# Adding the residual by TensorE and moving the softplus by one unit in a four-layer selective-scan kernel

## The chip, the cores and the metric

The kernel runs on one core of a Trainium2 chip as one program. The metric is the device time of that program in microseconds, the median of several executions. Besides the times there is one execution taken with the hardware profiler, and every duration below is of that one.

## The reference, cut to what matters

The input is a batch of 8 images with 192 channels and 56 x 56 points. Four layers follow each other, each `x = x + layer(group_norm(x))`. Layer 0 is an involution, layer 1 three narrow selective scans per image, and layers 2 and 3, which the change touches, one wide selective scan each:

```
xz = in_proj(group_norm(x));  x_in, z = split(xz)          # 384 channels each
xc = silu(conv4(x_in) + conv_b)                            # causal, along the points
dt, B, C = split(x_proj(xc));  dt = softplus(dt_proj(dt) + b)
h[d,n,t] = exp(dt[d,t]*A[d,n]) * h[d,n,t-1] + dt[d,t]*xc[d,t]*B[n,t]     # n < 16
y[d,t]   = sum_n C[n,t]*h[d,n,t] + D[d]*xc[d,t]
x = x + out_proj(y * silu(z))
```

## The kernel before, in words

**Jobs and units.** An image is cut into 7 chunks of 448 points. In layers 2 and 3 one chunk is one *job*, so there are 56 jobs in each. A job has 3 groups of 128 channels (j), and a group has 4 *units* (q), so 12 units, numbered 0 to 11 here (m in the code). A unit works on a tile `uhg` of 128 partitions x 4 x 449 numbers and takes these steps, each on its own engine:

- `decays` (L764): ScalarE writes exp(dt*A) into PSUM, in two halves of 2 activations. Each half has one buffer, so the decays of unit k+1 wait for the scan of the same half of unit k.
- the *product* dt*xc*B: by VectorE (`inputs_by_vector`, L792), which reads B from a PSUM tile that TensorE spreads (`spread_b`, L752), or by GpSimd (`inputs_by_pool`, L785), which reads B from a tile `rows` that a DMA brings (`row_in`, L649). `pool_units` says which units GpSimd has; in layers 2 and 3 these are 1, 3, 7, 9 and 11, and VectorE has the other seven.
- two *scans* (L796), one per half, on VectorE.
- the *readout* (L805): GpSimd multiplies the states by C. `keep` (L800) and `inputs_begin` (L772) carry the last state over on ScalarE.
- `reduce` (L814): TensorE adds up over n; at the first unit of a group also L811 (D*xc). After a group VectorE multiplies by the gate (`gated`, L830).

**The order.** Nothing is scheduled by a tool: the loop over units in `ssm_layer` writes each engine's order by hand. In iteration k VectorE does scan (k, 0), the product of k+1, scan (k, 1); GpSimd is given the product of k+2 and then the readout of k-2; TensorE is given the reduction of k-3 first. So the engines work on different units at the same time, each strictly in its own order. In unit 4 VectorE also does the product of unit 6 (`switches`).

**The background work.** What the next job needs is laid into 24 *places* of the running job, two for each unit: place 2m runs ahead of scan (m, 0) and place 2m+1 ahead of scan (m, 1). `places` spreads each list of steps evenly over a stretch of places by their costs; `bounds` gives the stretches. The input and convolution matmuls (L1136, L1168) stand in places 0 to 7; the block that swaps ScalarE's function table, does the two silus and swaps back (L616, L597, L589) in place 8; then the output projection of the job before (`after`, L1188) with the residual add on VectorE (L1194), and the projection to dt, B and C (L621, evicted by L625 and L626); the deltas (L655, L660) and the split of B into bf16 parts (L632, L633, L637) in places 10 to 13; in place 14 the softplus block, again between two table loads (L663, L589). The matmuls L667 bring xc into PSUM, VectorE makes dt*xc with them (`dtx`, L670), and `store` (L674) sends both to DRAM. From place 18 on come the write of the finished chunk, the normalization of the next and the gate matmuls. A *step* has matmuls and a rest; the rest waits in a list until a later step flushes it. Where a unit has little of this, TensorE is given matmuls of zeros (`nothing`, L820).

**The DMA queue.** All DMAs of these layers are issued by SyncE, in one order. A group's operands are fetched back from DRAM with each row repeated four times, by four DMAs (`load_ops`, tile `rep`, L742). They wait for the store of that group to land (`ops`, L674). The three `rows` of the next job that GpSimd's products need (`row_in(0, 1..3)`) are issued in units 9, 10 and 11, at the start of the iteration:

```
row_in(0, m - (per_job - NQ))      # before: rows 1, 2, 3 in units 9, 10, 11
```

In layers 2 and 3 that places the first of them on SyncE's queue behind the store of group 0 of the next job, its four `rep` loads and the stores of groups 1 and 2. The tiles `rows` and `rep` have 4 and 2 buffers.

**PSUM.** The general matmul tiles (`mm_tile`) have two buffers; B, y and each half of the decays have their own.

Of the kernel before, what the change touches and what calls it, by code (L numbers as in the profile page):

```python
# [18 lines left out]
CP = 96  # L19
NCT = 2  # L20
RC = 8
T = RC * WW
# [17 lines left out]
class Step:  # L40


    def __init__(self, matmuls, rest, left, cost=None, block=False):
        self.matmuls, self.rest, self.left, self.block = matmuls, rest, left, block
        self.cost = cost if cost is not None else 1.0 if matmuls else 0.3
        self.closes = block
        self.settles = False


def pause(cost=1.0):  # L50
# [36 lines left out]
def conv_mamba_stack(ctx: ExitStack, tc: tile.TileContext, a, out):  # L87
    nc = tc.nc
# [15 lines left out]
    def mm_tile():  # L104
        return banks.mm.tile([128, 512], F32, tag="mm", name="mm")
# [16 lines left out]
    ident = const([128, 128], a["ident"])  # L122
# [589 lines left out]
    def ssm_layer(pool, w, jobs, n_slots):  # L712


        nd = w.nd
        units = [(i, j, q) for i in range(len(jobs)) for j in range(nd) for q in range(NQ)]
        groups = [(i, j) for i in range(len(jobs)) for j in range(nd)]
        per_job = nd * NQ

        def pool_units(i):  # L720

            if nd == 4:
                last = i + 1 == len(jobs)
                if jobs[i][0] == 0:
                    return {1, 3, 5, 7, 9, 11, 13, 15} if last else {1, 3, 6, 7, 10, 11, 13, 15}
                return {1, 3, 7, 9, 11, 13, 15} | ({5} if last else set())
            return {1, 3, 7, 9, 11} | ({6} if i + 1 == len(jobs) else set())

        pool_rows = (1, 2, 3)
        us = [Layer() for _ in jobs]  # L730
# [102 lines left out]
        def bounds(job):  # L833

            silu = 8 if nd == 3 else 6
            softplus = silu + (6 if nd == 3 else 8 if job[0] == 1 else 12)
            copies = silu + (4 if nd == 4 else 2)
            return (0, silu), (silu, silu + 2), (silu + 2, copies), (copies, softplus), (softplus, softplus + 1), (softplus + 2, softplus + 4), (softplus + 4, n_places)

# [46 lines left out]
        for k, (i, j, q) in enumerate(units):  # L886
            m = k % per_job
            if m == 0:

                fetch, outs, rest = tail  # L890
                if i + 1 < len(jobs):
                    u = us[i + 1]
                    at = bounds(jobs[i + 1])
                    stretches = *jobs[i + 1][2](u, us[i], outs), rest + jobs[i + 1][3](u)
                    plan = places(*((steps, *p) for steps, p in zip(stretches, at)))
                else:
                    gates = Step(None, lambda: with_gates(lambda: None, us[i]), 0, 0.3, block=True)
                    plan = places(([gates], 4, 6), (outs + rest, 8, n_places))
                plan[3][:0] = [Step(None, fetch, 2, 0.0)]

            if i + 1 < len(jobs) and m - (per_job - NQ) in pool_rows:
                us[i + 1].row_in(0, m - (per_job - NQ))
            if i and m < NQ:
                us[i].row_in(1, m)
            if k >= NQ + 3 and q == 3:
                gated(k // NQ - 1)
            switches = i + 1 < len(jobs) and m == at[1][0] // 2
            melts = nd == 4 and i + 1 < len(jobs) and jobs[i][0] == 0 and m == at[4][0] // 2
            opens = nd == 4 and k >= 3 and units[k - 3][2] == 0
            more = 3 - math.ceil(load_of(plan[2 * m] + plan[2 * m + 1]))  # L910
            if opens:
                bg.run(plan[2 * m])
            if k >= 3 and not melts:
                reduce(k - 3)
                nothing(k - 3, more > 2)
            if not opens:
                bg.run(plan[2 * m])
            if not melts:
                nothing(k - 3, more > 0)
            load_when_free(k)  # L920
            scan(k, 0)
            if k + 1 < n_units:
                decays(k + 1, 0)
            if k + 3 < n_units:
                inputs_begin(k + 3)
            if k + 2 < n_units:
                inputs_by_pool(k + 2)
            if k >= 2:
                readout(k - 2)
            if k + 1 < n_units:  # L930
                inputs_by_vector(k + 1)
            if nd == 3 and k + 2 < n_units:
                spread_b(k + 2)
            if nd == 4 and (switches or melts):
                spread_next_b(k + 1)
            if melts:
                reduce(k - 3)
                nothing(k - 3, (more > 2) + (more > 0))
            bg.run(plan[2 * m + 1])
            if nd == 4:  # L940
                spread_next_b(k + 1)
            nothing(k - 3, more > 1)
            load_when_free(k)
            scan(k, 1)
            if (switches or melts) and k + 2 not in by_pool:
                inputs_by_vector(k + 2)
            keep(k)
            if k + 1 < n_units:
                decays(k + 1, 1)
            if m == per_job - 1:  # L950
                tail = jobs[i][4](us[i])
# [174 lines left out]
    def dense_jobs(pool, w, layer):  # L1126
        jobs = []
        chunks = Chunks(pool, layer)
        cks = chunks.all
        for ck in cks:  # L1130
            c = ck.c

            def in_mm(m, ck=ck):
                pm = mm_tile()
                for k in range(NCT):
                    nc.tensor.matmul(  # L1136
                        pm[:, :T], lhsT=w.inw[:, k, m * 128 : (m + 1) * 128], rhs=ck.v[:, k, :],
                        start=(k == 0), stop=(k == NCT - 1),
                    )
                return pm  # L1140

            def norm(ck=ck):
                def gnorm():
                    ck.v = chunks.normalized(ck, "v", 2)

                return [Step(None, gnorm, 2), Step(None, lambda: chunks.fetch_next(ck), 2)]

            ck.norm = norm

            def prepare(u, *beside, c=c, ck=ck, in_mm=in_mm):  # L1150
                xps = {}

                def xin(j):
                    xps[j] = in_mm(j)

                def xin_out(j):
                    if j == 0:
                        ck.xin = pool.tile([128, w.nd, T + 3], F32, tag="xin", name="xin", bufs=2)
                        if c == 0:
                            nc.gpsimd.memset(ck.xin[:, :, 0:3], 0.0)  # L1160
                        else:
                            nc.scalar.copy(ck.xin[:, :, 0:3], cks[ck.place - 1].xin[:, :, T : T + 3])
                    evict(w, ck.xin[:, j, 3:], xps[j][:, :T], j)

                def conv_mm(j):
                    pm = mm_tile()
                    for k in range(4):
                        nc.tensor.matmul(pm[:, :T], lhsT=w.convd[:, j, k, :], rhs=ck.xin[:, j, k : k + T], start=(k == 0), stop=(k == 3))  # L1168
                    return pm

                convs, *others = project_steps(pool, w, u, conv_mm, 4, *beside)
                return (
                    (ck.norm() + [pause()] if ck.place == 0 else [])
                    + [Step(lambda j=j: xin(j), lambda j=j: xin_out(j), 1 if j else 0, 2) for j in range(w.nd)]
                    + convs, *others,
                )

            def gates(u, ck=ck, in_mm=in_mm):
                normed = cks[ck.place + 1].norm() if ck.place + 1 < len(cks) else []
                return normed + gate_steps(pool, w, u, lambda j: in_mm(w.nd + j), 2)  # L1180

            def after(u, ck=ck):
                ops = {}

                def out_proj(t):
                    ops[t] = mm_tile()
                    for j in range(3):
                        nc.tensor.matmul(  # L1188
                            ops[t][:CP, :T], lhsT=w.outw[:, j, t * CP : (t + 1) * CP], rhs=u.zs[:, j, :],
                            start=(j == 0), stop=(j == 2),  # L1190
                        )

                def add(t):
                    nc.vector.tensor_add(ck.x[:, t, :], ck.x[:, t, :], ops[t][:CP, :T])  # L1194

                return (
                    lambda: chunks.fetch_again(ck), [Step(lambda t=t: out_proj(t), lambda t=t: add(t), 1, 3) for t in range(NCT)],
                    [pause()] + chunks.leave_steps(ck),
                )

            jobs.append((0, c == 0, prepare, gates, after))
        return jobs

# [86 lines left out]
```

## Time and profile before

| what | us |
|---|---|
| median of 3 runs | 24391.19 |
| lowest, highest | 24375.81, 24401.58 |
| the profiled execution, its time | 24428.22 |
| its span (first to last instruction) | 24426.4 |
| VectorE busy | 23026.9 (94%) |
| GpSimd busy | 22738.4 (93%) |
| TensorE busy | 20547.5 (84%) |
| ScalarE busy | 17006.8 (70%) |
| layer 2, from 16705 to 20627 | 3922, of which VectorE 3674.7, GpSimd 3555.5, TensorE 3285.8, ScalarE 2892.3 busy |
| layer 3, from 20627 to 24407 | 3780, of which VectorE 3594.9, GpSimd 3545.4, TensorE 3243.2, ScalarE 2839.3 busy |

The profile gives busy time per engine, the costliest groups of instructions with what ended the idle time before them, the chain of work that ended last, and the DMA queues. The trace behind it can be asked for a timeline of one engine, for groups of instructions in a stretch of time, and for who waited for whom. An f32 matmul stands in it as two records. In the names, `uhg<-rep,rows` means that the instruction writes uhg and reads rep and rows; DVE is VectorE, ACT ScalarE, POOL GpSimd, PE TensorE, SPq SyncE's queue.

### The profile page before, as it was taken

Reading aid. Unit: us, or ns where it says so; the run is one execution under the profiler, and the core shown is the slowest. Engines: PE = TensorE matmul, PEld = TensorE weight load, DVE = VectorE, ACT = ScalarE, POOL = GpSimd, SP = SyncE. Lnnn points to the kernel's source line nnn. Section 1 sums busy time; section 2 is a strip of 40 time slices with the busy share of each in tenths; the row PEclk is TensorE's granted clock in tenths of the full one; section 3 lists DMA queues with packets and bytes.
Section 4 is the critical chain, followed back from the end, with each engine's and each line's share of the span. In section 5 each row is a group of like instructions: output and inputs, shape, how many; then the busy total and the mean of one; then the engine's idle time right before and its main releaser. Section 6 shows DMA issues by size and latency. Waiting matters only on the chain.

```text
span 24426.4 us, 238439 instructions
## 1 busy us (share of the span) xinstructions
PE 20547.5 (84%) x74445; PEld 6487.3 (27%) x74445; DVE 23026.9 (94%) x15882; ACT 17006.8 (70%) x32578; POOL 22738.4 (93%) x6775
## 2 busy tenths in 40 slices
PE   8988888888888888888888888888888887888888
PEld 2222222222222222222222222222333332333332
DVE  8989999999999999999999999997999998999999
ACT  2137777777777777777777777776777776777777
POOL 5669999999999999999999999997999998999999
PEclk9987888878887887887887887878989898999998
DMA  4433333333333333333333333333444443444443
GB/s 111 109 106 131 128 126 133 127 127 130 132 128 126 131 128 125 132 130 125 130 128 126 130 130 128 128 129 111 140 141 142 141 139 123 142 144 144 142 143 129
DMA packets 1209092, 3171.55 MB, mean 130 GB/s; under 512 B 166444, under 2 KB 470596, under 8 KB 1207688
## 3 DMA queue, kind: packets, MB, share of 16 engines
q1 hardware_dynamic: 1205016, 3155.25, 39.4%
q8 instruction: 584, 9.57, 0.2%
q14 instruction: 692, 5.67, 0.1%
q10 hardware_dynamic: 2800, 1.06, 0.0%
HBM read 2438.45 MB, written 555.55 MB: 123 GB/s over the span
## 4 chain that ended last, share of the span: by engine, by line
DVE 35%; PE 29%; ACT 14%; issue 11%; POOL 6%; DMA 5%; SPq 1%; DVEq 0%; POOLq 0%; ACTq 0%
DVE uhg L796 22%; DVE uhg L792 8%; ACT da L764 6%; PE y L814 4%; POOL uhg L805 4%; DMA rows<-bc 3%; PE mm L1110 3%; PE mm L1168 3%; PE mm L655 2%; PE mm L1080 2%; PE mm L621 2%; POOL uhg L785 2%; PE mm L429 2%; ACT dt L663 1%; PE y L820 1%
## 5 line engine op out<-in xcount | busy, mean ns | idle before, releaser
L796 DVE TENSOR_TENSOR_SCAN uhg<-da,uhg 128x898 f32<-128x898 f32 x8064 | 15913.4, 2011 | 606.9 <-ACT da L764 586.1
L805 POOL TENSOR_TENSOR uhg<-uhg,rows 128x1792 f32<-128x1792 f32 x4032 | 14730.5, 3674 | 283.6 <-ACT carry L800 267.4
L764 ACT ACTIVATE da<-rep,k 128x448 f32<-128x448 f32 x16128 | 10262.3, 636 | 1436.8 <-DVE uhg L796 1064.1
L785 POOL TENSOR_TENSOR uhg<-rep,rows 128x1792 f32<-128x1792 f32 x1795 | 7160.6, 3989 | 784.6 <-DMA rows<-bc 435.6
L814 PE MATMUL y<-uhg,k 128*32 128x448 f32 x32256 | 4516.4, 634 | 343.1 <-POOL uhg L805 341.4
L792 DVE TENSOR_TENSOR uhg<-rep,b 128x1792 f32<-128x1792 f32 x2237 | 4469.6, 1998 | 180.2 <-PE b L752 132.4
L800 ACT COPY carry<-uhg 128x4 f32<-128x4 f32 x4032 | 784.5, 195 | 3506.5 <-DVE uhg L796 3427.8
L820 PE MATMUL y<-w_d,k 128*128 128x448 f32 (+1 forms) x5280 | 2490.5, 575 | 0.0
L811 PE MATMUL y<-xc,w_d 128*128 128x448 f32 x2016 | 1533.4, 856 | 1091.2 <-DVE zs L830 1091.1
L1098 PE MATMUL mm<-xs,k 64*128 64x448 f32 x1344 | 875.4, 755 | 773.5 <-ACT zs L694 587.5
L655 PE MATMUL mm<-dbl,w_dt 36*128 36x448 f32 (+1 forms) x2016 | 1319.6, 753 | 222.4 <-ACT k L637 222.4
L814 PEld LDWEIGHTS y<-uhg,k 128*32 128x32 f32 x32256 | 679.9, 114 | 3093.6 <-issue 1935.2
L820 PEld LDWEIGHTS y<-w_d,k 128*128 128x128 f32 x5280 | 1023.1, 210 | 1645.0 <-issue 1618.3
L1136 PE MATMUL mm<-v,w_in 96*128 96x448 f32 x2688 | 1284.0, 612 | 80.3 <-ACT zs L696 36.8
L752 PE MATMUL b<-k,k 96*128 96x448 bf16 x2237 | 852.2, 381 | 446.5 <-DVE uhg L792 446.3
L1080 PE MATMUL mm<-xs,k 128*128 128x448 f32 x2688 | 1155.1, 571 | 26.3 <-ACT zs L694 11.3
L667 PE MATMUL mm<-xc,k 128*128 128x448 f32 x2016 | 1033.1, 630 | 84.4 <-DVE dt L670 84.4
L1168 PE MATMUL mm<-xin,w_conv 128*128 128x448 f32 x2688 | 1088.6, 547 | 1.4 <-ACT xin L696 0.8
L441 DVE TENSOR_TENSOR prod<-mm,shifted 128x448 f32<-128x448 f32 x1680 | 930.0, 613 | 152.5 <-PE mm L429 77.0
L811 PEld LDWEIGHTS y<-xc,w_d 128*128 128x128 f32 x2016 | 470.7, 270 | 1941.0 <-DVE zs L830 1375.2
L449 POOL TENSOR_TENSOR x<-x,one 96x448 f32<-96x448 f32 x560 | 630.7, 1134 | 265.3 <-DVE one L441 247.8
L621 PE MATMUL mm<-xc,w_x 128*36 128x448 f32 (+1 forms) x2016 | 816.4, 546 | 10.5 <-ACT xc L616 10.5
(138 smaller groups left out, 19388.1 us busy)
## 6 DMA issues: line engine op xcount, KB each, us to landing
rep<-ops SPq DMA_DIRECT2D x4032, 448.0 KB, 5.8
ops<-dt SPq DMA_DIRECT2D x1008, 448.0 KB, 3.2
rows<-bc SPq DMA_DIRECT2D x1960, 224.0 KB, 6.3
shifted<-xpad SPq DMA_DIRECT2D x672, 179.0 KB, 4.5
xg<-stream SPq DMA_DIRECT2D x168, 336.0 KB, 7.7
xr<-stream SPq DMA_DIRECT2D x168, 336.0 KB, 7.0
stream<-xr SPq DMA_DIRECT2D x112, 336.0 KB, 7.5
xs<-xg SPq DMA_DIRECT2D x224, 112.0 KB, 2.3
```

The lines of the kernel that those rows point to most:

```text
L621: nc.tensor.matmul(u.ps[:nk, :T], lhsT=w.xproj[:, j, :], rhs=u.xc[:, j, :], start=(j == 0), stop=(j == nd - 1))
L655: nc.tensor.matmul(u.dps[j][:, :T], lhsT=w.dtw[:, j * 128 : (j + 1) * 128], rhs=u.dbl[:nk, :], start=True, stop=True)
L764: nc.scalar.activation(t[:, 64 + 449 * r : 512 + 449 * r], reps[k // NQ][:, 2 * h + r, 0, :], AF.Exp, scale=w.neg_a[:, j * NR + 2 * h + r, ...
L785: nc.gpsimd.tensor_mul(uhg[k][:, :, 1:], reps[k // NQ][:, :, 1, :], b)
L792: nc.vector.tensor_mul(uhg[k][:, :, 1:], reps[k // NQ][:, :, 1, :], b)
L796: nc.vector.tensor_tensor_scan(v, banks.da[h][:, 63:961], v, 0.0, ALU.mult, ALU.add)
L805: nc.gpsimd.tensor_mul(v, v, us[i].rows[1, q].unsqueeze(1).to_broadcast([128, NR, T]))
L811: nc.tensor.matmul(ys[k // NQ][:, :T], lhsT=w.dd[:, j, :], rhs=us[i].xc[:, j, :], start=True, stop=False)
L814: nc.tensor.matmul(y[32 * r : 32 * r + 32, :T], lhsT=fold, rhs=uhg[k][:, r, 1:], start=False, stop=(q == NQ - 1))
L820: nc.tensor.matmul(ys[k // NQ][:, : nd * 112], lhsT=zeros, rhs=w.dd.rearrange("p j e -> p (j e)")[:, : nd * 112], start=False, stop=False,)
L1080: nc.tensor.matmul(pm[:, :T], lhsT=w.inconv[:, k, j * 128 : (j + 1) * 128], rhs=ck.xs[:, i, 2 - 2 * k : 2 - 2 * k + T], start=(k == 0), st ...
L1168: nc.tensor.matmul(pm[:, :T], lhsT=w.convd[:, j, k, :], rhs=ck.xin[:, j, k : k + T], start=(k == 0), stop=(k == 3))
```

## The change

In layers 2 and 3 alone:

- The residual is added by TensorE: two matmuls of `ident` with the chunk (f32, 96 x 96 x 448) open the two PSUM tiles of the output projection, at the start of place 8 (`ahead`), and ScalarE copies the finished tiles out (`leave`) where VectorE added before. For the last job, which nothing follows, they stand in `out_proj`.
- The softplus block goes from place 14 to place 16, that is from unit 7 to unit 8. The deltas and the split of B now have places 10 to 15. The products with xc and the stores follow in places 18 and 19 (before 16 and 17), and the last stretch begins with place 20.
- GpSimd has the product of unit 10 and VectorE that of unit 9 (before the other way round).
- `row_in` of the next job is called one unit earlier, in units 8, 9 and 10. By that the first two rows stand on SyncE's queue ahead of the store of group 0 and the `rep` loads, and the third behind the stores.

What follows from the planner: 209 more matmuls of zeros over the two layers, about two per job, since the deltas are spread more thinly.

```diff
-            return {1, 3, 7, 9, 11} | ({6} if i + 1 == len(jobs) else set())
+            return {1, 3, 7, 10, 11} | ({6} if i + 1 == len(jobs) else set())
...
-            softplus = silu + (6 if nd == 3 else 8 if job[0] == 1 else 12)
+            softplus = silu + (12 if nd == 4 and job[0] != 1 else 8)
...
                 plan[3][:0] = [Step(None, fetch, 2, 0.0)]
-
-            if i + 1 < len(jobs) and m - (per_job - NQ) in pool_rows:
-                us[i + 1].row_in(0, m - (per_job - NQ))
+                if outs and outs[0].ahead:
+                    plan[8][:0] = [Step(None, outs[0].ahead, 0, 0.0)]
+
+            row = m - (per_job - NQ) + (nd == 3)
+            if i + 1 < len(jobs) and row in pool_rows:
+                us[i + 1].row_in(0, row)
...
+                def residual():
+                    for t in range(NCT):
+                        ops[t] = mm_tile()
+                        nc.tensor.matmul(ops[t][:CP, :T], lhsT=ident[:CP, :CP], rhs=ck.x[:, t, :], start=True, stop=False)
+
                 def out_proj(t):
-                    ops[t] = mm_tile()
+                    if not ops:
+                        residual()
                     for j in range(3):
                         nc.tensor.matmul(
                             ops[t][:CP, :T], lhsT=w.outw[:, j, t * CP : (t + 1) * CP], rhs=u.zs[:, j, :],
-                            start=(j == 0), stop=(j == 2),
+                            start=False, stop=(j == 2),
                         )
 
-                def add(t):
-                    nc.vector.tensor_add(ck.x[:, t, :], ck.x[:, t, :], ops[t][:CP, :T])
-
+                def leave(t):
+                    nc.scalar.copy(ck.x[:, t, :], ops[t][:CP, :T])
+
+                outs = [Step(lambda t=t: out_proj(t), lambda t=t: leave(t), 1, 3) for t in range(NCT)]
+                outs[0].ahead = residual
```

## The prediction

> **What bounds the kernel now.** I read the busy times first, then the groups of layer 3 (20627 to 24348 us) by engine, then the timelines of one job of layer 3, engine by engine. On the page no engine is full:
>
> ```profile
> PE 20547.5 (84%) x74445; PEld 6487.3 (27%) x74445; DVE 23026.9 (94%) x15882; ACT 17006.8 (70%) x32578; POOL 22738.4 (93%) x6775
> ```
>
> Layer 3 takes 3780 us for 56 jobs, 67.5 each; VectorE is busy for 64.2 of them and GpSimd for 63.3. The groups say where each is idle (columns: count | busy us, mean ns | idle us before them and what ended it):
>
> ```profile
> L805 POOL TENSOR_TENSOR uhg<-uhg,rows 128x1792 f32<-128x1792 f32 x659 | 2405.9, 3676 | 12.0 <-ACT carry L800 11.7
> L785 POOL TENSOR_TENSOR uhg<-rep,rows 128x1792 f32<-128x1792 f32 x277 | 1107.6, 3999 | 282.8 <-DMA rows<-bc 168.5 <-DMA rep<-ops 60.2 <-DMA xg<-stream 36.4
> ```
>
> GpSimd never waits for a scan; it waits once per job, for a DMA. The timeline shows where (start, duration, instruction, idle before it):
>
> ```profile
> 22716.32 3.99 POOL L785 TENSOR_TENSOR uhg<-rep,rows 128x1792 f32<-128x1792 f32 x1 [4.81 <-DMA rows<-bc]
> 22720.26 7.30 POOL L805 TENSOR_TENSOR uhg<-uhg,rows 128x1792 f32<-128x1792 f32 x2
> 22727.53 3.99 POOL L785 TENSOR_TENSOR uhg<-rep,rows 128x1792 f32<-128x1792 f32 x1
> 22731.48 14.56 POOL L805 TENSOR_TENSOR uhg<-uhg,rows 128x1792 f32<-128x1792 f32 x4
> ...
> 22783.73 3.98 POOL L785 TENSOR_TENSOR uhg<-rep,rows 128x1792 f32<-128x1792 f32 x1 [4.02 <-DMA xg<-stream]
> ```
>
> The product that waits is that of unit 1 of the next job; I call its start G. From G to G is 67.41 us, the job. SyncE's queue shows what it waits for: the operands are stored, fetched, and only then is the row issued, at 22774.99.
>
> ```profile
> 22768.31 0.34 SPq L674 DMA_DIRECT2D ops<-dt  x1
> 22770.83 2.46 SPq L742 DMA_DIRECT2D rep<-ops  x4
> 22773.39 1.55 SPq L674 DMA_DIRECT2D ops<-dt  x2
> 22774.99 0.72 SPq L649 DMA_DIRECT2D rows<-bc  x1
> ```
>
> By the trace's landings, averaged over layer 3, this row lands at 60.5 us of a job and G follows 0.2 to 0.3 later; the fourth rep copy lands at 57.7, 11.85 after the first dtx ended. So the bound is a loop of three legs, told by VectorE's line:
>
> ```profile
> 22739.59 2.02 DVE L792 TENSOR_TENSOR uhg<-rep,b 128x1792 f32<-128x1792 f32 x1 [0.25 <-PE b L752]
> ...
> 22751.54 0.61 DVE L1194 TENSOR_TENSOR xr<-xr,mm 96x448 f32<-96x448 f32 x1
> 22752.08 2.02 DVE L796 TENSOR_TENSOR_SCAN uhg<-da,uhg 128x898 f32<-128x898 f32 x1
> 22754.01 0.59 DVE L1194 TENSOR_TENSOR xr<-xr,mm 96x448 f32<-96x448 f32 x1
> ...
> 22761.89 2.03 DVE L796 TENSOR_TENSOR_SCAN uhg<-da,uhg 128x898 f32<-128x898 f32 x1 [1.00 <-ACT da L764]
> ...
> 22767.68 1.13 DVE L670 TENSOR_TENSOR dt<-dt,mm 128x448 f32<-128x448 f32 x2
> ```
>
> - Leg 1, G to VectorE's product of unit 4: 22716.32 to 22739.59, **23.3**. GpSimd does G, the readouts of 9 and 10, the product of 3 and the readout of 11; TensorE then reduces unit 11, does a convolution and spreads B for unit 4, for which VectorE waits.
> - Leg 2, that product to the end of the first dtx: 22739.59 to 22768.3, **28.7**.
> - Leg 3, dtx to G: store, fetch, row, 22768.3 to 22783.73, **15.4**. Sum 67.4, the job.
>
> **The change, leg by leg.** Leg 1: neither GpSimd's order from G to the readout of 11 nor TensorE's in units 0 to 2 changes: 23.3.
>
> Leg 3: the first row is issued ahead of the store and lands long before. What is left is the store and the four rep loads. dtx, store and loads keep their order, so G follows the first dtx by 11.85 plus the 0.2 to 0.3: **12.1**, 3.3 less. From both sides: section 6 of the page gives medians of 3.2 (ops) and 5.8 (rep) to landing, with 0.3 of issue 9.3 at the least; 15.4 if the loads become no quicker than the row was.
>
> Leg 2, in steps:
>
> - Softplus and dtx one unit later: unit 8 now lies ahead of the first dtx, two scans and a product (VectorE now has unit 9 there, so the decays of 9 behind the 3.9 us softplus block stay covered). A scan and a product take 1.93 from start to start: 3 x 1.93 = **+5.8**.
> - Two adds off VectorE: 0.54 + 0.52 from start to start. The first half is held by ScalarE: the decays of unit 5 behind the silu block end at 22751.52, when the product of 6 ends too; both adds go, **-1.0**.
> - The 1.00 before scan (7, 0) goes: before, three evictions (L637 and two of L660) stand ahead of its decays; after, none: **-1.0**.
> - The two identity matmuls. They stand ahead of the spread of B for 6 and of the output projection on TensorE. Their like is not in the trace at that shape; between L1188 (0.39 a record) and L632 (0.46), four records are 1.6 to 1.8. Their cover is TensorE's wait of 0.66 there (the bracket of this line of its timeline). So the output projection and L621 end about 1.0 later:
>
> ```profile
> 22747.83 0.35 PE L752 MATMUL b<-k,k 96*128 96x448 bf16 x1 [0.66 <-DVE uhg L792]
> ```
>
> - ScalarE copies L621's result at 22755.46 before, 0.4 after the matmul's end of 22755.07; after at about 22756.3. Behind this copy in its queue stand L626, keep and the decays of (6, 1), which end 2.5 later, at 22758.8. VectorE, 1.0 ahead by now, wants that scan at 22757.4: **+1.35**. The copies that replace the adds (about 0.52, by L625) stand in ScalarE's wait for TensorE and cost nothing themselves. From both sides: 0 if TensorE is not late, 2.4 if the copies lie behind it in full.
> - After that no wait is left: the deltas are evicted ahead of need, softplus ends near 22771.3 and VectorE reaches dtx at 22772.9.
>
> Leg 2 is 28.7 + 5.8 - 1.0 - 1.0 + 1.35 = **33.85**. The loop is 23.3 + 33.85 + 12.1 = **69.25**, 1.85 more than before. The change takes 1.2 us of work from VectorE and shortens leg 3, but puts a whole unit on the leg that closes the loop.
>
> 112 jobs x 1.85 = 207. Layer 2 runs the same loop; its 70.0 per job hold the group norm at the end of an image (some 5 us for each of 8). VectorE will then have slack ahead of leg 1's end, which hides part of that: I take 20 off. The 209 zero matmuls lie in TensorE's waits: 0, at most 0.37 x 2 per job where they do not. So +185, on the profiled execution 24428 + 185 = 24613. That execution was 37 us above the median of the runs; on the median, **24575**.
>
> **A rule against it.** At 22776.14, after 2.02 us of idle time, TensorE's reduction of eight records takes 1.72 us, elsewhere 0.96. The Trainium skill, "TensorE: Matmul & The Clock Gate", section "What's actually happening", says that an idle window of some 3.4 us halves the clock until as long a busy one. The trace's granted clock agrees: 0.5 for 10.2 or 13.7 us at a time near the end of most jobs. By the trace's rows alone the sum stays as above; by the rule it is that of the third rival, if TensorE waits that long ahead of the reduction of unit 9.
>
> **Rivals.**
>
> - *TensorE is not late* (the identities hide, or the ScalarE copies do): leg 2 is 32.5, the loop 67.9, +0.5 x 112 - 20 = +36: 24427, no change. For it: VectorE waits on TensorE for little in layer 3 (57.5 us before L792). Against: from 22735 to 22762 TensorE has no other gap than the 0.66. Chance 0.16.
> - *The loads come quicker, faster than before.* If leg 3 is 9.3, the sum of the medians, the loop is 66.45, and the job 0.95 shorter than before; -0.95 x 112 - 20 = -126: 24265. It decides from a leg 3 under 67.4 - 23.3 - 33.85 = 10.25. Against: in this trace the same chain, with an empty queue ahead, took 11.85. Chance 0.13.
> - *The clock.* GpSimd's wait grows to 69.25 - 63.4 = 5.9, TensorE idles before it reduces unit 9 and comes back at half clock: reduction, four matmuls and the spread (0.96 + 3.27 + 0.35) take more: nothing at the least, 3.7 at the most (all of it longer by 1.72/0.96); I take 2.2, since the clock returns midway. VectorE's product of 2 then holds the loop instead, about 1.8 more per job, if TensorE's lead gained there is not given back: +390: 24780. Chance 0.11.
> - The change does what it says; the rows' earlier issue is in SyncE's order. The likeliest case keeps 0.60.
>
> **How the numbers follow.** Within 0.2% (49 us, about what a measurement of this kernel can tell) lies the first rival; the forecast and the clock lie above. Faster 0.13, same 0.16, slower 0.71. The range takes in the first rival and most of the clock's case and leaves out the faster one: 24380 to 24720.
>
> **What would show it.** GpSimd's wait for unit 1's product stays, ended by rep and not rows, near 5.9 per job; VectorE's idle time moves to the product of unit 2 (3 to 4 us) and scan (6, 1) (over 1); the gap before scan (7, 0) is gone; L670 starts 5 later in the job. If GpSimd's wait shrinks below 3 per job, leg 3 was wrong and the kernel is faster.

## The result and the profile after

The changed kernel takes 24626.5 us (median of 4 runs) against 24392.6 for the kernel before: 1.0097 times as long, 95% interval 1.0085 to 1.0110. It is slower by 234 us; 184 were forecast (24575). The profiled execution grew from a span of 24426.4 to 24627.8, by 201. No engine is full: TensorE is busy 329 us more, but at 85% of the span, and VectorE, the busiest, 107 us less:

```profile
PE 20876.9 (85%) x75311; PEld 6649.4 (27%) x75311; DVE 22920.3 (93%) x15658; ACT 17083.8 (69%) x32802; POOL 22750.5 (92%) x6775
```

The groups of layer 3 (20700 to 24400 us) show whose idle time grew: first GpSimd's, then VectorE's. Columns are count, busy us, mean ns, idle us before them and what ended it:

```profile
L806 POOL TENSOR_TENSOR uhg<-uhg,rows 128x1792 f32<-128x1792 f32 x631 | 2307.0, 3676 | 75.9 <-ACT carry L801 75.6
L786 POOL TENSOR_TENSOR uhg<-rep,rows 128x1792 f32<-128x1792 f32 x264 | 1054.2, 3993 | 285.8 <-DMA rep<-ops 250.8 <-issue 35.0
```

```profile
L797 DVE TENSOR_TENSOR_SCAN uhg<-da,uhg 128x898 f32<-128x898 f32 x1266 | 2498.8, 2011 | 67.0 <-ACT da L765 66.4
L793 DVE TENSOR_TENSOR uhg<-rep,b 128x1792 f32<-128x1792 f32 x369 | 739.8, 2005 | 293.7 <-PE b L753 270.5 <-DMA rep<-ops 15.1 <-issue 5.6
```

GpSimd's wait before its products is now ended by `rep`, where it was `rows`. VectorE waits 294 us before its products, nearly all of it for B, about 5.5 per job, where it waited 74 in the kernel before:

```profile
L792 DVE TENSOR_TENSOR uhg<-rep,b 128x1792 f32<-128x1792 f32 x386 | 773.5, 2004 | 74.0 <-PE b L752 57.5 <-DMA rep<-ops 15.5
```

One job's GpSimd timeline, from one product of unit 1 to the next, 70.36 us apart:

```profile
22781.68 3.98 POOL L786 TENSOR_TENSOR uhg<-rep,rows 128x1792 f32<-128x1792 f32 x1 [5.99 <-issue]
22785.62 7.29 POOL L806 TENSOR_TENSOR uhg<-uhg,rows 128x1792 f32<-128x1792 f32 x2
...
22852.04 3.97 POOL L786 TENSOR_TENSOR uhg<-rep,rows 128x1792 f32<-128x1792 f32 x1 [5.02 <-DMA rep<-ops]
```

SyncE's queue in that job: two rows stand far ahead of the store, and what lands last before 22852.04 is the fourth rep copy.

```profile
22825.50 1.17 SPq L650 DMA_DIRECT2D rows<-bc  x2
22840.33 0.34 SPq L675 DMA_DIRECT2D ops<-dt  x1
22842.84 2.46 SPq L743 DMA_DIRECT2D rep<-ops  x4
```

VectorE in the same job: the products of units 2 and 4, scan (6, 1), and the first two dtx.

```profile
22796.94 2.02 DVE L793 TENSOR_TENSOR uhg<-rep,b 128x1792 f32<-128x1792 f32 x1 [5.67 <-PE b L753]
...
22807.10 1.99 DVE L793 TENSOR_TENSOR uhg<-rep,b 128x1792 f32<-128x1792 f32 x1
...
22825.69 2.03 DVE L797 TENSOR_TENSOR_SCAN uhg<-da,uhg 128x898 f32<-128x898 f32 x1 [0.80 <-ACT da L765]
...
22839.71 1.12 DVE L671 TENSOR_TENSOR dt<-dt,mm 128x448 f32<-128x448 f32 x2
```

So the three legs of this job are 25.4 (22781.68 to 22807.10), 33.2 (to the end of the first dtx at 22840.3) and 11.7 (to 22852.04). Averaged over the 51 middle jobs of a layer, in us, with GpSimd's wait at the end of leg 3 as "wait" (the legs always add up to the job, whatever binds; that they bind is seen by the wait):

| kernel | layer 3: leg 1 + 2 + 3 = job | wait | layer 2: job | whole kernel, ratio to before |
|---|---|---|---|---|
| before | 23.5 + 29.1 + 15.0 = 67.5 | 4.0 | 68.7 | 1 |
| predicted | 23.3 + 33.85 + 12.1 = 69.25 | 5.9 | 1.85 more, less 20 us in all | 1.0075 |
| changed | 24.9 + 33.3 + 12.0 = 70.1 | 5.4 | 69.8 | 1.0097 |

From the job times, 56 x (70.1 - 67.5) + 56 x (69.8 - 68.7) is 207, close to the 201 by which the spans differ.

### The profile page after: what moved, and what is told of

It is laid out like the page before. It is cut to its first block, busy times and chain, and to the rows that moved or that the text cites. A ratio compares the mean times of both kernels' runs of the same rounds, so it can differ in the third digit from the quotient of the medians.

```text
span 24627.8 us, 240244 instructions
## 1 busy us (share of the span) xinstructions
PE 20876.9 (85%) x75311; PEld 6649.4 (27%) x75311; DVE 22920.3 (93%) x15658; ACT 17083.8 (69%) x32802; POOL 22750.5 (92%) x6775
## 4 chain that ended last, share of the span: by engine, by line
DVE 32%; PE 30%; issue 12%; ACT 11%; POOL 9%; DMA 5%; SPq 1%; DVEq 0%; POOLq 0%; ACTq 0%
DVE uhg L797 20%; DVE uhg L793 7%; POOL uhg L806 6%; PE y L815 5%; ACT da L765 5%; DMA rep<-ops 4%; POOL uhg L786 3%; PE mm L1114 3%; PE mm L622 3%; PE mm L1084 2%; PE mm L656 2%; PE y L821 2%; PE mm L1140 1%; PE mm L430 1%; PE mm L668 1%
## 5 line engine op out<-in xcount | busy, mean ns | idle before, releaser
L801 ACT COPY carry<-uhg 128x4 f32<-128x4 f32 x4032 | 782.8, 194 | 3260.2 <-DVE uhg L797 3159.5
L821 PE MATMUL y<-w_d,k 128*128 128x448 f32 (+1 forms) x5698 | 2644.8, 569 | 0.0
L821 PEld LDWEIGHTS y<-w_d,k 128*128 128x128 f32 x5698 | 1096.9, 209 | 1745.1 <-issue 1698.5
L1140 PE MATMUL mm<-v,w_in 96*128 96x448 f32 x2688 | 1390.4, 656 | 32.2 <-ACT zs L697 15.5
L661 ACT ACTIVATE dt<-mm,k 128x448 f32<-128x448 f32 x1008 | 621.2, 626 | 350.1 <-PE mm L656 349.8
```

The costliest lines, as they stand in the source:

```text
L821: nc.tensor.matmul(ys[k // NQ][:, : nd * 112], lhsT=zeros, rhs=w.dd.rearrange("p j e -> p (j e)")[:, : nd * 112], start=False, stop=False,)
L1140: nc.tensor.matmul(pm[:, :T], lhsT=w.inw[:, k, m * 128 : (m + 1) * 128], rhs=ck.v[:, k, :], start=(k == 0), stop=(k == NCT - 1),)
```

## The experiments

The theory is the loop of the prediction: GpSimd's product of unit 1, its next readouts, TensorE, VectorE's product of unit 4, VectorE to dtx, store and rep loads, and back. The rivals: that the residual on TensorE and ScalarE is what costs; that VectorE's work binds; that the rows matter; that the clock has no part. All but e2 are the changed kernel with an edit; e2 is the kernel before with one. Each was timed in three rounds; ratios are to the kernel before on the same chip.

**e4: all of the change but the residual.** VectorE adds again, as in the kernel before.

```diff
-                    if not ops:
-                        residual()
+                    ops[t] = mm_tile()
...
-                            start=False, stop=(j == 2),
+                            start=(j == 0), stop=(j == 2),
...
-                    nc.scalar.copy(ck.x[:, t, :], ops[t][:CP, :T])
+                    nc.vector.tensor_add(ck.x[:, t, :], ck.x[:, t, :], ops[t][:CP, :T])
...
-                outs[0].ahead = residual
```

> The changed kernel with the residual added by VectorE as before; softplus in unit 8, the swap and the early rows stay. Theory: the second leg gets 1.0 of adds and loses the 0.8 wait before scan (6, 1): 24627 to 24690 us. Rival (the residual on TensorE is the cost): about 24400.

24633.4 us, ratio 1.0108 (1.0093 to 1.0123). The residual is not what makes the change slow: without it the loss is as large. Leg 2 is 33.7 against 33.3: the adds (1.0) against the wait of 0.8 before scan (6, 1), about as expected.

**e1: softplus back in unit 7, and the swap of units 9 and 10 undone with it.**

```diff
-            return {1, 3, 7, 10, 11} | ({6} if i + 1 == len(jobs) else set())
+            return {1, 3, 7, 9, 11} | ({6} if i + 1 == len(jobs) else set())
...
-            softplus = silu + (12 if nd == 4 and job[0] != 1 else 8)
+            softplus = silu + (6 if nd == 3 else 8 if job[0] == 1 else 12)
```

> The changed kernel with its softplus block back in unit 7 and GpSimd's units as before (9, not 10); the residual on TensorE and the early rows stay. Theory (a loop from GpSimd's product of unit 1 over VectorE, softplus, store and rep loads back to it): the whole unit leaves the loop, 24.5 + 28.5 + 12.2 = 65.2 us or less per job, so VectorE with 63.0 of work and some 3 of waits binds: 66 per job, 24190 us (24130 to 24260), faster than both kernels; GpSimd's wait for unit 1 falls under 3 us. Rival (the work added on TensorE and ScalarE by the residual is the cost): no better than 24580. Rival (the swap of units 9 and 10 costs): as the theory, so this run alone does not tell it apart.

24431.3 us, ratio 1.0021 (1.0011 to 1.0030). Most of the loss is gone; leg 2 is 29.5 and GpSimd's wait 2.0 in layer 3, so the loop is open. The run undoes the softplus and the swap together; e12, below, undoes the swap alone. But the gain of 200 us over the kernel before did not come; the expectation was wrong about what binds next. With the loop open VectorE waits for ScalarE's decays, 208.3 us in layer 3:

```profile
L797 DVE TENSOR_TENSOR_SCAN uhg<-da,uhg 128x898 f32<-128x898 f32 x1323 | 2611.0, 2011 | 208.3 <-ACT da L765 204.9 <-POOL uhg L806 3.4
```

By place in the job the largest waits are 0.8 before scan (6, 1), 1.85 before (7, 0) and 0.86 before (8, 0); the last was there in the kernel before (0.8), as were 1.1 before (7, 0). The decays of (7, 0) stand on ScalarE behind evictions of the deltas, which wait for TensorE, and TensorE has hardly a gap from unit 1 to unit 7 (0.28 in the job looked at). It is the residual that pushes these late: e7, with the residual alone, has the same waits before (6, 1) and (7, 0), while e2, without it, has none before (6, 1) and 1.1 before (7, 0).

**e7: the residual alone.** e1 with the rows late as well, so that the residual is the one part of the change that is left.

```diff
-            row = m - (per_job - NQ) + (nd == 3)
+            row = m - (per_job - NQ)
```

> The kernel before with one part of the change alone: the residual on TensorE and the copies on ScalarE; softplus in unit 7, GpSimd's units and the rows as before. Theory: the second leg loses 1.0 of adds and gains waits of 0.8 before scan (6, 1) and 0.75 before scan (7, 0), as the run with softplus back showed; the loop is 67.4 + 0.5: 24390 to 24500 us. Rival (VectorE's work binds, so 1.06 less per job is a gain): 24270.

24477.5 us, ratio 1.0036 (1.0023 to 1.0049). As expected, by itself the residual costs: 90 us, with leg 2 longer by 0.5 in layer 3. Taking 1.2 us of adds a job from an engine that is 94% busy made the kernel slower.

**e2: the early rows alone**, in the kernel before.

```diff
-            if i + 1 < len(jobs) and m - (per_job - NQ) in pool_rows:
-                us[i + 1].row_in(0, m - (per_job - NQ))
+            row = m - (per_job - NQ) + (nd == 3)
+            if i + 1 < len(jobs) and row in pool_rows:
+                us[i + 1].row_in(0, row)
```

> The kernel before with one part of the change alone: the rows of the next job are fetched one unit earlier. Theory: the first row lands before the rep copies, so the third leg falls from 15.4 to 12.1 and the loop to 64.1; VectorE, with 64.2 of work and some 2.2 of waits, binds at 66.4: -1.1 x 112 = 24270 us (24220 to 24330); GpSimd's wait before unit 1 falls from 4.4 to 3 or less. Rival (the row was no bound, the fetched operands were): 24392, no change.

24343.9 us, ratio 0.9983 (0.9974 to 0.9992): faster than before, but less than expected. Leg 3 falls from 15.0 to 11.9 and GpSimd waits for `rep`:

```profile
L785 POOL TENSOR_TENSOR uhg<-rep,rows 128x1792 f32<-128x1792 f32 x273 | 1088.6, 3988 | 102.0 <-DMA rep<-ops 90.2 <-issue 10.5 <-POOL uhg L805 0.9
```

Layer 3's job is 66.4, the expected number. Layer 2's fell by 0.2 alone (68.7 to 68.5); the expectation had taken layer 2 to be as layer 3. Why layer 2 gains less was not tried.

**e3: the rows late, in the changed kernel** (the edit of e7 alone).

> The changed kernel with the rows fetched in units 9, 10 and 11 as before. Theory: since the store of group 0 is now in unit 9 and the row is issued at the start of that unit, the first row still stands ahead of the store on SyncE's queue; the loop is the same: 24627 us (24580 to 24680). Rival (the early rows are what shortened the third leg): 3.2 more per job, 24985.

24608.7 us, ratio 1.0095 (1.0080 to 1.0110): no difference. With the store in unit 9 the first row stands ahead of it either way.

**e9: the rows behind the store**, in the changed kernel.

```diff
-            if i + 1 < len(jobs) and row in pool_rows:
+            if i + 1 < len(jobs) and row in pool_rows and nd == 4:
                 us[i + 1].row_in(0, row)
+            if i + 1 < len(jobs) and nd == 3 and m >= 10:
+                for r in (1, 2) if m == 10 else (3,):
+                    us[i + 1].row_in(0, r)
```

> The changed kernel with the first two rows of the next job issued in unit 10, behind the store and the rep loads as in the kernel before. Theory (the third leg ends with whichever lands last): it goes from 12.3 back to about 15.4, 3.1 x 112: 24970 us (24900 to 25020), and GpSimd's wait is ended by the row again. Rival (the third leg is not on the loop): 24627.

24995.6 us, ratio 1.0247 (1.0230 to 1.0265), as expected. In layer 3 leg 3 is 14.9, leg 2 as in the changed kernel, leg 1 longer by 0.5 (25.4), the job 73.7, and what ends the wait has changed back:

```profile
L786 POOL TENSOR_TENSOR uhg<-rep,rows 128x1792 f32<-128x1792 f32 x247 | 984.9, 3987 | 464.2 <-DMA rows<-bc 228.1 <-DMA out<-xr 141.2 <-DMA rep<-ops 59.1
```

A delay put on leg 3 alone comes out in the whole time: 369 us, where leg 3 by itself gives 2.9 x 112 = 325. That it is more goes with leg 1: GpSimd's wait grows to 8.4, and behind it TensorE is at half clock for longer. That is the loop, shown by its edge.

**e5: TensorE kept busy**, with six matmuls of zeros in its wait at the end of unit 11.

```diff
+            if nd == 3 and m == per_job - 1:
+                nothing(k - 3, 6)
             if m == per_job - 1:
```

> The changed kernel with six more matmuls of zeros at the end of unit 11 of layers 2 and 3, in TensorE's wait for the readout of unit 9. Theory (1.2 of the first leg's growth is TensorE at half clock after that wait): the first leg goes back from 24.5 to 23.3, part of it given back at scan (6, 1): 24500 to 24560 us, and the granted clock at 3 to 10 us of a job rises towards 1. Rival (the clock has no part in it): 24627 or slower by the added matmuls.

24557.9 us, ratio 1.0069 (1.0054 to 1.0084), 69 us less than the changed kernel's median. In layer 3 leg 1 falls from 24.9 to 23.5, the job from 70.1 to 68.8, and the granted clock over the layer rises from 0.92 to 0.96. In layer 2 the job does not get shorter (69.9). This is what it mends, in the changed kernel's TensorE timeline: a wait of 3.87 for the readout of unit 9, the reduction still quick, then eight records at half clock:

```profile
22789.34 0.96 PE L815 MATMUL y<-uhg,k 128*32 128x448 f32 x8 [3.87 <-POOL uhg L806]
22790.23 6.30 PE L1140 MATMUL mm<-v,w_in 96*128 96x448 f32 x8
22796.32 0.58 PE L753 MATMUL b<-k,k 96*128 96x448 bf16 x1
```

The same work in the kernel before:

```profile
22723.99 0.96 PE L814 MATMUL y<-uhg,k 128*32 128x448 f32 x8 [0.32 <-POOL uhg L805]
22725.45 3.27 PE L1136 MATMUL mm<-v,w_in 96*128 96x448 f32 x8 [0.51 <-ACT zs L694]
22728.56 0.35 PE L752 MATMUL b<-k,k 96*128 96x448 bf16 x1
```

And with the matmuls of zeros in the wait (e5):

```profile
22734.51 4.12 PE L821 MATMUL y<-w_d,k 128*128 128x336 f32 x14
22738.74 0.96 PE L815 MATMUL y<-uhg,k 128*32 128x448 f32 x8
22739.62 3.27 PE L1142 MATMUL mm<-v,w_in 96*128 96x448 f32 x8
```

In the changed kernel the work behind the wait takes 3.0 longer, so the spread of B for unit 2 is late by that too, and VectorE's product of unit 2 waits for it. What counts is where the half clock falls, not the layer's mean, which was lower in the kernel before (0.90): from 8 to 12 us after GpSimd's product of unit 1, averaged over the jobs of layer 3, TensorE is at half clock for 0.09 of the time in the kernel before, 0.91 in the changed one and 0.14 in e5.

"TensorE: Matmul & The Clock Gate" of the Trainium skill ("What's actually happening") gives an idle window of some 3.4 us for the gate, free-running. The lengths agree: of 103 half-clock stretches in layer 3 of the changed kernel, 56 last 3.4 us and 31 last 6.8. But here a drop did not take a window that was idle throughout: in the 3.4 us up to the drop at 22790.30, TensorE waited for 2.45 and worked for 0.96, and in the kernel before, up to the drop at 22776.17, it waited for 2.0 and worked for 1.4. So the half clock can begin after the wait, on the work behind it.

**e6: GpSimd's first product one unit later.** The changed kernel with unit 2 on GpSimd and unit 1 on VectorE.

```diff
-            return {1, 3, 7, 10, 11} | ({6} if i + 1 == len(jobs) else set())
+            return {2, 3, 7, 10, 11} | ({6} if i + 1 == len(jobs) else set())
```

> The changed kernel with GpSimd's product of unit 1 given to VectorE and that of unit 2 to GpSimd, the rest as changed. Theory (the loop is closed at GpSimd's first product of a job): the first leg now begins one readout later in GpSimd's order, 3.6 less, and TensorE idles less, so the loop falls to 65 to 66.5 and VectorE (63.0 of work and 2 to 3 of waits) binds: 24150 to 24260 us, faster than both kernels. Rival (TensorE and ScalarE in units 3 to 8 bind, as with softplus back in unit 7): 67.2 per job, about 24310. Rival (which unit GpSimd has does not matter): 24627.

24240.3 us, ratio 0.9938 (0.9923 to 0.9953): as expected, and faster than both kernels. No work is taken from any engine; the readout of unit 9 now stands ahead of the product that waits for the loads, so leg 1, which now begins at the product of unit 2, is 20.3, the job 65.5 in layer 3 (67.5 in layer 2), and GpSimd's wait falls to 1.6 per job:

```profile
L786 POOL TENSOR_TENSOR uhg<-rep,rows 128x1792 f32<-128x1792 f32 x268 | 1071.5, 3998 | 85.0 <-DMA rep<-ops 71.7 <-issue 13.2
```

**e11: e6 with the residual on VectorE** (the edits of e4 and e6 together).

> The run with GpSimd's product of unit 2, but with the residual added by VectorE as before. Theory: the loop is as long as with the residual on TensorE (the adds of 1.0 against the wait of 0.8 before scan (6, 1)), 65.5 to 65.8 per job, so 24240 to 24290 us. Rival (with the loop opened VectorE's work binds, so the residual on TensorE is worth its 1.06 per job): 24360.

24275.9 us, ratio 0.9959 (0.9944 to 0.9974). As expected, 65.5 per job in layer 3 too. Where the residual is added is worth at most little even here; the intervals of e6 and e11 overlap, and what they differ by lies in layer 2 (68.3 per job against 67.5).

**e12: the swap undone.** GpSimd has unit 9 again and VectorE unit 10.

```diff
-            return {1, 3, 7, 10, 11} | ({6} if i + 1 == len(jobs) else set())
+            return {1, 3, 7, 9, 11} | ({6} if i + 1 == len(jobs) else set())
```

> The changed kernel with GpSimd's product of unit 9 and VectorE's of unit 10 as before; the rest as changed. Theory: the product of unit 9 on VectorE lies on the second leg, between softplus' start and dtx; without it dtx waits for the softplus instead, some 1.4 earlier than now: 24627 - 1.4 x 112 = 24470 us (24420 to 24540), and VectorE waits some 3 before scan (9, 0), off the loop. Rival (the product is cover for the softplus block, as its place suggests, and without it the block stands in the open): 24627 to 24850.

24452.1 us, ratio 1.0033 (1.0021 to 1.0044), as expected. In the changed kernel the product of unit 9 is cover for the softplus block, but cover that lies on the loop; without it leg 2 is 32.4 in layer 3. More of the gain there is leg 1, which the expectation did not name: it falls to 23.4, and the half clock from 8 to 12 us after GpSimd's product of unit 1 to 0.06 of the time. The loop stays closed, at 67.9, with GpSimd waiting 4.4 a job for the loads:

```profile
L786 POOL TENSOR_TENSOR uhg<-rep,rows 128x1792 f32<-128x1792 f32 x272 | 1088.3, 4001 | 240.5 <-DMA rep<-ops 193.3 <-issue 32.6 <-DMA ops<-dt 10.6
```

VectorE waits 1.5 before scan (9, 0) then, not the 3 expected. So of the 0.97% that the change lost, the swap alone takes back 0.64 points, and e1, which puts the softplus back as well, 0.76: with the residual on TensorE, leaving the softplus late costs little more. What made the change slow is mostly the product of unit 9 that the swap puts ahead of the first dtx, on the loop that the later softplus keeps closed.

**e13: unit 2 on GpSimd and the swap undone.**

```diff
-            return {1, 3, 7, 10, 11} | ({6} if i + 1 == len(jobs) else set())
+            return {2, 3, 7, 9, 11} | ({6} if i + 1 == len(jobs) else set())
```

> The run with GpSimd's product of unit 2, and with its product of unit 9 in place of 10. Theory: the loop gets shorter still, about 64.1, and no longer binds; VectorE (63.0 of work) now pays the wait before scan (9, 0) in full, 66 per job: 24230 to 24310 us, no better than the run with unit 2 alone (24240). Rival (the loop still binds at 65.5): 24100.

24411.3 us, ratio 1.0010 (1.0001 to 1.0020): slower than e6, the expected sign, and by more than expected. Layer 3 has 66.7 per job, near the 66 expected; layer 2 has 69.7, and why was not tried. GpSimd hardly waits for the loads any more, 5.8 us in the layer, but for the copy that follows VectorE's scans (L801), and the scans wait for the decays. Of their 3.0 per job the largest part, 1.5, is before scan (9, 0), behind the softplus block:

```profile
L806 POOL TENSOR_TENSOR uhg<-uhg,rows 128x1792 f32<-128x1792 f32 x664 | 2429.6, 3676 | 171.4 <-ACT carry L801 171.4
L786 POOL TENSOR_TENSOR uhg<-rep,rows 128x1792 f32<-128x1792 f32 x276 | 1104.0, 4000 | 5.8 <-DMA rep<-ops 3.4 <-issue 1.4 <-POOL uhg L806 1.0
```

```profile
L797 DVE TENSOR_TENSOR_SCAN uhg<-da,uhg 128x898 f32<-128x898 f32 x1326 | 2615.0, 2012 | 166.3 <-ACT da L765 166.3
```

So the same swap costs with the loop closed (e12 against the changed kernel) and pays where the loop no longer binds (e6 against e13).

## Why the prediction was right

The loop held in every experiment, and the time came out 50 us above the forecast. The term that was mis-sized is leg 1, and that the sum came so near is in part luck, as a later point says.

- **What bounds.** The loop, not an engine. Shown from four sides: a delay on leg 3 costs at least its full size (e9), a product taken off leg 2 gains 0.9 a job there and more in leg 1 (e12), the softplus put back with it opens the loop (e1), and a first product later in GpSimd's order opens it at leg 1 (e6).
- **Leg 3**, forecast 12.1, was 12.0. The forecast's reason, the row ahead of the store, was right; that the earlier call of `row_in` does it was not. e3 shows that the late softplus alone already puts the row ahead. In the kernel before, the earlier call does it (e2).
- **Leg 2**, forecast 33.85, was 33.3. The unit on the loop (+5.8) and the gone wait before scan (7, 0) are there. The unit's product stood in the forecast as cover for the softplus block; that the kernel is faster without it (e12) was not seen. The wait before scan (6, 1) was forecast at 1.35 and is 0.80; the forecast's own figures, added up again, give some 1.5. It kept 0.4 between the end of L621 and the copy of its result, but in the changed trace the copy (L626) starts 0.04 after the matmul's end. The identity matmuls take 1.74 for four records (1.6 to 1.8 forecast) and ScalarE's copies stand in its wait, as said: 0.47 of that wait is left ahead of L626:

```profile
22820.93 2.45 PE L622 MATMUL mm<-xc,w_x 128*44 128x448 f32 x6
22823.42 0.53 ACT L626 COPY dbl<-mm 44x448 f32<-44x448 f32 x1 [0.47 <-PE mm L622]
```

- **Leg 1**, forecast at 23.3 unchanged, is the term that was mis-sized: 24.9 in layer 3, up 1.4 from the kernel before. The forecast asked only whether an engine's order changes in that leg, and not whether its work takes as long behind a longer wait. That is the third rival's mechanism, which the prediction gave 0.11 and 1.8 us a job; e5 takes 1.4 away again. It came on top of the forecast rather than in its place, and leg 1 grew in layer 3 alone. The prediction also read the clock of the kernel before amiss: of its 88 half-clock stretches in layer 3, 26 last 10.2 or 13.7 us, and the most common length is 6.8 (37).
- **VectorE's slack.** The wait before the product of unit 2, forecast at 3 to 4, is 5.0 in layer 3; with the clock mended (e5) it is 2.6. L671 starts 8.4 later in a job counted from its first scan, not 5: the new wait stands between, and the forecast's own 3 to 4 for it was left out of the 5.
- **Layer 2** was taken to grow as layer 3 less 20 us. It grew by 1.1 a job: leg 1 by -0.2 (24.9 to 24.6), leg 2 by 4.5 and leg 3 by -3.1, so the two layers part at leg 1. The slack is there: the first two jobs of an image take 2.2 more than two others, where it was 5.9, so it hides 3.7 per image, 30 us in all. TensorE was at half clock in layer 2 as well, for 0.60 of the time from 8 to 12 us after GpSimd's product of unit 1. In e5 it is 0.10, and still the job is no shorter: leg 1 falls by some 0.4 in most jobs and rises by 2.2 in the second of each image. Why was not tried.
- **The sum** came near in part by luck. A job of layer 3 grew by 0.75 more than forecast, a job of layer 2 by as much less. And of the 50 us, 33 are in the runs that were profiled: the one before lay 36 us above the median of its runs, which the forecast took off, the one after lay 3 above. Between these two executions it was 201 us against the 185 forecast.
- **The first rival** (TensorE not late) and the second (loads quicker) fell: the wait before scan (6, 1) is there, and leg 3 is 12.0, near the chain's 12.1 and not the 9.3 of the medians.

## What to carry to other kernels

When two engines are at 93 and 94% and neither is full, look for a loop through both: follow the one wait that comes back once per iteration, add up the legs until they make the period, and price an edit by what it does to the legs, not to the busy engine. Work taken off the busiest engine can cost (e7), and cover for a stall costs while it lies on a loop that binds (e12) and pays where none does (e13). The cheapest mend is often order: put in front of the instruction that waits whatever on its engine doesn't need what it waits for (e6), which gained 0.6% here.

## What the runs showed of the hardware

TensorE's clock fell to half 0.96 us after a wait of 3.87 us had ended, and the eight matmul records behind the first reduction took 6.30 us in place of 3.27. Matmuls of zeros in the wait raised the granted clock of layer 3 from 0.92 to 0.96 and shortened the kernel, although they add 672 matmuls (6 x 112). Of the four rep copies of 448 KB of a job's first group, issued within 2.5 us, the first landed 3.3 to 3.6 us and the fourth 7.0 to 7.2 us after its own issue (medians of layer 3 in each run); nothing that was moved on the queue ahead of their store or behind them changed that (leg 3 was 11.9 to 12.1 in layer 3 wherever the first row was ahead of the store and GpSimd waited for the loads).
